# The stages ahead of the expert loop, rearranged: context scaling by halves, order of exponential and weight steps, layer norms moved to ScalarE

## The chip, the core and the metric

The kernel runs on one core of a Trainium2 chip, as one launch. The metric is device time in microseconds (us) of one execution; three executions of the kernel before took 943.69, 947.76 and 951.05 us, median 947.76. TensorE (PE) does matmuls and transposes; VectorE (DVE), ScalarE (ACT) and GpSimd (POOL) do the elementwise work; SyncE (SP) issues transfers (DMA). Each engine works through its own instructions in the order written, and a transfer is queued on the engine that issues it.

## The reference, cut to what matters

`x` is 16 sequences of 256 positions by 256 channels (4,096 rows); `ctx` is 16 sequences of 120 positions by 256 channels. In short, with `LN` a layer norm:

```
h0  = LN(x)
z   = LN(ctx @ W_in + b_in) * g_ln + beta_ln
h   = silu(pe @ Wp1 + bp1) @ Wp2 + bp2            # a filter per channel, 512 taps
w   = exp(-l * exp(a))                            # the window, l = 0..511
cv  = causal_conv(w * h, z) over 512 positions, every second one kept: 256
xr  = h0 + silu(LN1(h0) @ W1a + b1a) @ W1b + b1b  # first MLP, 256 -> 512 -> 256
y   = xr * cv
x   = x + tanh(g_xattn) * (y + silu(LN2(y) @ W2a + b2a) @ W2b + b2b)   # second MLP
h   = LN(x) @ Wm + bm, cut into heads of 32
g   = the two largest of softmax(head @ emb), over 16 experts
out = sum over those two of g * (gelu(head @ W1[e] + b1[e]) @ W2[e] + b2[e])
x   = x + tanh(g_ffn) * (out @ Wo + bo)
```

The reference does the convolution with Fourier transforms, and its result is in fp32.

## The kernel before, in words

**Precision.** The fp32 factors of a product are split into two parts of a faster format: `hi`, a rounded copy, and `lo`, the rest (`f - hi`). A product is three matmuls (hi·hi, hi·lo, lo·hi). Splitting a weight or an activation is therefore one copy and one subtraction; names such as `nt_hi`/`nt_lo`, `s_hi`/`s_lo`, `w_hi`, `v_hi` are these parts.

**Order.** From the start up to `tc.manual_schedule()` (L956) a scheduler with a model of the engines places the instructions; from there on each engine gets them in the order in which the program writes them. Generators are used to interleave: a function yields after each piece, `some(gen, n)` runs the next `n` pieces of it, `whole` runs the rest.

**Front (to 58 us).** Loads go out on the queues of SyncE and ScalarE: `load_ctx` (L623) brings the four pieces of the context, `bc` (L643) holds all row biases, copied to every partition. The exponential of `a`, the two tanh gates and the window follow (L706 to L711), then the filter's small MLP (L712 to L736), which goes to memory as `filt_d`, from where SyncE's `load_hankel` fetches Hankel tiles (`hk`, 1.07 MB each, three buffers). `Context(half).product()` (L752) multiplies eight of the 16 sequences by W_in: four tiles for each half, each with four of the 32 slices (a slice, called a row in what follows, is half the positions of one sequence) and a matmul by `pick_z` for the bias, sums of squares on ScalarE, and a scaling by g_ln on VectorE (Y, `z_sb`). `context_root` (L778) forms the reciprocal root `rz` of all 32 rows, and `context_norm` (L783) scales the 32 rows into `zn`: the first 12 by a ScalarE copy and a GpSimd add, the other 20 each by one operation on VectorE.

**First MLP and convolution (55 to 185 us).** The 4,096 rows are eight jobs (`Mlp1`) of 512. A job has `norms`, `prep` (`prep_n`, the normed rows, and `prep_x`), `turn` (transposes, then the split into `nt_hi`, `nt_lo`), `first` (four tiles: matmuls L205, ScalarE's silu L260, `s_lo` by L268, on VectorE for the last two tiles and on GpSimd for the first two) and `second` (matmuls, from L278; its first one in each job's bias is L293). The convolution is 16 steps: `conv_mm` (64 matmuls L901, two copies `cvs` L908) and `conv_turn` (transposes, and the product with `xr`). `mlps1` (L1057) interleaves, through `mixed` (L1047): at each piece of a job one piece of `weights`, and at every second piece one of `side`, the convolution:

```python
side, weights, since = conv(), chain(early_roots(2, 3), early_roots(3, XB), early_weights(), early_roots(XB, NB)), 0
```

XB is 5 and NB is 8. `early_roots` (L817) takes statistics and roots of the x tiles of later jobs; `early_weights` shifts and splits the second MLP's weights W2a (`w2`) and W2b (`v2`), the tiles x2 to x4 and both weights being loaded on GpSimd's queue behind `m0.first`.

**Up to the experts (142 to 254 us).** `Mlp2` jobs of 512 rows (`prep` L340) and `Route` jobs (`prep` L400, which computes the experts' inputs and gates; `shift`, `lay` and `fetch` carry them through memory into the layout of the experts). Both norm their rows by `normed` (L178): with an `off` on ScalarE, else on VectorE; both have called it without one. `behind_it` (L1167) is the order of the last of this: it spreads `late_weights` (the experts' W1 into `wst`, with two ScalarE copies and two GpSimd subtractions L1038; then the load of Wo into a shared stage, and its split), `routes[1]` and `mlps[2]` over jobs 6 and 7 of the first MLP.

**Expert loop (254 to 945 us).** For each block of rows, TensorE multiplies by W1 (`hps`, L1259), ScalarE applies gelu (`hid`, L1264), TensorE multiplies by W2 (`eo`, L1274), VectorE weights by the gate (`part`, L1282), GpSimd adds (`comb`, L1284). In between stand the second MLP's and the routes' remaining jobs.

Of the kernel before, what the change touches and what calls it, by code (L numbers as in the profile page):

```python
# [24 lines left out]
FP = mybir.dt.float32  # L25
# [8 lines left out]
P = 128  # L34
# [11 lines left out]
NB = 8  # L46
# [47 lines left out]
def block_kernel(  # L94
# [151 lines left out]
    def first(job, bank, w, b, bh, by_table):  # L246

        job.s = []
        for m in range(NM):
            ps = bank("first")  # L250
            project(ps, job, w, m)
            if job.room:
                hi, lo, f = job.room(m)
            else:
                hi, lo = pair(s_in[0], "s", [P, TB], s_in[1])
                f = base.tile([P, TB], FP, name="silu", tag="silu", bufs=2)
            job.s.append((hi, lo))
            if by_table:
                nc.scalar.activation(hi, ps, AF.Silu, bias=b[:, m : m + 1])  # L259
                nc.scalar.activation(f, ps, AF.Silu, bias=b[:, m : m + 1])  # L260
            else:

                nc.scalar.activation(f, ps, AF.Tanh, bias=bh[:, m : m + 1], scale=0.5)
                nc.vector.tensor_scalar(f, f, 0.5, 0.5, ALU.mult, ALU.add)
                nc.vector.scalar_tensor_tensor(f, ps, b[:, m : m + 1], f, ALU.add, ALU.mult)
                nc.vector.tensor_copy(hi, f)
            eng = nc.vector if by_table and m >= NM // 2 else nc.gpsimd
            eng.tensor_tensor(lo, f, hi.bitcast(FP), ALU.subtract)  # L268
            yield 6 * TB
# [47 lines left out]
    class Mlp2:  # L317


        def __init__(self, i, room=None):  # L320
            self.i, self.room = i, room

# [17 lines left out]
        def prep(self, pool=base, name="n"):  # L340
            t0 = 4 * self.i
            self.n = pool.tile([P, 4, D], FP, name=name, tag=name)
            normed(self.n, Y[:, t0 : t0 + 4, :], mv2, t0, self.r)

# [44 lines left out]
    class Route:  # L389
# [9 lines left out]
        def prep(self):  # L399
            t0 = 4 * self.i  # L400
            y = Y[:, t0 : t0 + 4, :]
            self.n = base.tile([P, 4, D], FP, name="n", tag="n")
            normed(self.n, y, mv3, t0, self.r)

# [133 lines left out]
    with ExitStack() as ph:  # L538
# [83 lines left out]

        def load_ctx(g):  # L623
            nc.scalar.dma_start(ctx_sb[g], ctx_r[:, :, bass.ts(g, 4 * P)])

# [14 lines left out]
        for g in (1, 2, 3):  # L640
            load_ctx(g)
        w1a = staged(W1a.rearrange("(c p) n -> p c n", p=P), 2, DFF, nc.sync)
        nc.scalar.dma_start(bc, rows.partition_broadcast(P))  # L643
        w1b = staged(W1b.rearrange("(c p) n -> p c n", p=P), NM, D, nc.sync)
# [59 lines left out]


        ea = scalar("a", AF.Exp)  # L706
        tgx = scalar("g_xattn", AF.Tanh)
        tgf = scalar("g_ffn", AF.Tanh)
        nea = const.tile([P, 1], FP, name="nea")
        nc.vector.tensor_scalar(nea, ea, -1.0, None, ALU.mult)  # L710
        nc.scalar.activation(window, window, AF.Exp, scale=nea)  # L711
        for m, n in enumerate((P, P, DPOS)):  # L712
# [64 lines left out]

        def context_root():  # L778
            var = bank("turn")[:, 0:32]
            nc.tensor.matmul(out=var, lhsT=both, rhs=ss, start=True, stop=True)  # L780
            return rsqrt_eps("rz", var, 32, pool=front)

        def context_norm(rz, by_pool=12):  # L783
            for n in range(32):
                b, k = n // 2, n % 2
                dst = zn[:, :, k, b : b + 2 * B + 1 : 2 * B]
                z, c = z_sb[:, n // 4, n % 4], rz[:, n : n + 1]
                shift = gz[:, 1].rearrange("p (r e) -> p r e", e=2)
                if n < by_pool:
                    nc.scalar.activation(z, z, AF.Copy, scale=c)  # L790
# [3 lines left out]
                else:  # L794
                    nc.vector.scalar_tensor_tensor(
                        dst, z.rearrange("p (r e) -> p r e", e=2), c, shift, ALU.mult, ALU.add
                    )


# [32 lines left out]
        class Mlp1:  # L832
            room = None

# [212 lines left out]
        def mixed(gen, n=9):  # L1047
            nonlocal since
            for _ in range(n):
# [3 lines left out]
                if since % 2 == 0:  # L1053
                    some(side)
                some(weights)

        def mlps1(first, last):  # L1057

            for n in range(first, last):
# [17 lines left out]
                if n < last - 1:  # L1077
                    soon.prep()
                else:
# [3 lines left out]
                    mlp20.stats()  # L1083
                mixed(ahead)
            mlp20.norms()

# [80 lines left out]
        def behind_it():  # L1167
# [447 lines left out]
```

## Time and profile before

| what | value |
| --- | --- |
| median of three executions | 947.76 us (943.69 to 951.05) |
| the profiled execution | 946.54 us, its span 944.7 us |
| TensorE matmul busy | 903.9 us (96%) |
| TensorE weight load busy | 491.3 us (52%) |
| VectorE busy | 713.5 us (76%) |
| ScalarE busy | 670.2 us (71%) |
| GpSimd busy | 566.4 us (60%) |
| transfers | 149.88 MB, mean 159 GB/s |
| mean granted TensorE clock | 0.986 |

All durations in what follows come from that one profiled execution, whose span is the time from the first to the last instruction. A busy engine isn't always one that limits: shares are means over stages, so the span is read stage by stage, and in each the question is which wait ends last. An operation is named by its line in the kernel before, its output tile and its inputs. "Granted clock" is the share of full speed that TensorE was given.

### The profile page before, as it was taken

What the parts mean: (1) busy time and instruction counts of PE and PEld (TensorE: products, weight loads), DVE (VectorE), ACT (ScalarE), POOL (GpSimd) and SP (SyncE); (2) the same over time, 40 slices, a digit from 0 to 9 for tenths busy, and PEclk for the clock granted to TensorE, in tenths of its full rate; (3) what the DMA queues carried; (4) which work ended last, traced back from release to release, by engine and by line L of the source; (5) the groups of instructions that cost most, each with busy time, mean ns of one, the idle gap of its engine ahead of it and who ended that gap; (6) DMA issues with size and microseconds to landing.
All of it is one profiled execution on the core that took longest, in us unless ns stands there. A gap on an engine that the chain in (4) does not pass through costs nothing.

```text
span 944.7 us, 16777 instructions
## 1 busy us (share of the span) xinstructions
PE 903.9 (96%) x6068; PEld 491.3 (52%) x6068; DVE 713.5 (76%) x1297; ACT 670.2 (71%) x856; POOL 566.4 (60%) x459
## 2 busy tenths in 40 slices
PE   6989999998889999999999999999999999989996
PEld 2767778787544544454544445454454444433433
DVE  5676447779978997898899789978985985693343
ACT  4553435585478778778877877887788778778883
POOL 3051222545467677776777777777767867486553
PEclk9999999999799999999999999999999999999998
DMA  7758970352457656947675686469465747746441
GB/s 241 167 155 218 228 203 16 76 137 69 120 134 182 154 149 177 232 128 179 187 198 144 169 213 161 133 188 240 113 182 171 187 127 197 185 117 179 123 123 45
DMA packets 88744, 149.88 MB, mean 159 GB/s; under 512 B 10251, under 2 KB 51723, under 8 KB 88655
## 3 DMA queue, kind: packets, MB, share of 16 engines
q1 hardware_dynamic: 85428, 141.08, 57.3%
q0 software_dynamic: 1296, 4.72, 1.7%
q10 hardware_dynamic: 1936, 3.02, 0.9%
q8 instruction: 48, 0.79, 0.4%
q14 instruction: 36, 0.29, 0.1%
HBM read 120.32 MB, written 28.46 MB: 157 GB/s over the span
## 4 chain that ended last, share of the span: by engine, by line
PE 58%; DVE 20%; DMA 9%; issue 5%; ACT 3%; SPq 2%; POOL 2%; POOLq 0%; ACTq 0%; DVEq 0%
PE hps L1259 20%; PE eo L1274 18%; PE aux L1318 5%; DVE part L1282 4%; DMA gates<-g_d 4%; DMA hk<-filt_d 3%; PE b_second L278 2%; PE b_first L205 2%; PE b_conv L901 2%; PE aux L205 2%; DMA t_d<-t_lo 2%; PE aux L1387 1%; DVE bn L170 1%; PE b_conv L205 1%; ACT hid L1264 1%
## 5 line engine op out<-in xcount | busy, mean ns | idle before, releaser
L1264 ACT ACTIVATE hid<-hps 128x1024 f32<-128x1024 f32 x512 | 512.1, 1025 | 145.0 <-PE hps L1259 132.2
L1284 POOL TENSOR_TENSOR comb<-comb,part 128x512 f32<-128x512 f32 x240 | 329.5, 1373 | 159.4 <-DVE part L1282 154.1
L1259 PE MATMUL hps<-stack,wst 98*128 98x512 f32 x1024 | 341.8, 425 | 2.8 <-ACT hid L1264 2.8
L1259 PEld LDWEIGHTS hps<-stack,wst 98*128 98x128 f32 x1024 | 162.3, 189 | 248.7 <-ACT hid L1264 120.2
L1274 PE MATMUL eo<-hid,w2s 128*32 128x512 f32 x2048 | 274.6, 608 | 7.9 <-DVE part L1282 6.7
L1282 DVE SCALAR_TENSOR_TENSOR part<-eo,cv,gates 128x512 f32<-128x512 f32 x237 | 175.4, 744 | 90.6 <-PE eo L1274 68.8
L1274 PEld LDWEIGHTS eo<-hid,w2s 128*32 128x32 f32 x2048 | 40.6, 108 | 102.9 <-issue 47.5
L268 POOL TENSOR_TENSOR s_lo<-silu,s_hi 128x512 fp32r<-128x512 f32 x18 | 23.0, 1289 | 71.7 <-ACT silu L260 45.0
L1377 POOL TENSOR_TENSOR s_lo<-silu,s_hi 128x512 fp32r<-128x512 f32 x24 | 31.0, 1292 | 33.6 <-DVE s_hi L1376 27.6
L1375 DVE SCALAR_TENSOR_TENSOR silu<-silu,u 128x512 f32<-128x512 f32 x24 | 26.1, 1087 | 22.5 <-ACT u L1372 22.5
L259 ACT ACTIVATE s_hi<-b_first,b1f 128x512 fp32r<-128x512 f32 x32 | 21.9, 684 | 26.0 <-PE b_first L205 25.4
L1409 DVE TENSOR_SCALAR n<-Y,mv,r_r 128x256 f32<-128x256 f32 x44 | 37.2, 886 | 3.0 <-POOL nt_lo L1433 3.0
L278 PE MATMUL b_second<-v_hi,s_hi 128*128 128x256 f32 x144 | 38.6, 300 | 0.0
L278 PE MATMUL b_second<-v_lo,s_hi 128*128 128x256 f32 x144 | 37.1, 289 | 0.0
L901 PE MATMUL b_conv<-hk,zn 60*32 60x256 f32 x1024 | 34.7, 379 | 1.9 <-ACT cvs L908 1.4
L1433 POOL TENSOR_TENSOR nt_lo<-n,nt_hi 128x512 fp32r<-128x512 f32 x26 | 33.6, 1292 | 3.1 <-DVE nt_hi L1432 3.1
L908 ACT COPY cvs<-b_conv 128x256 f32<-128x256 f32 x32 | 10.5, 376 | 30.2 <-PE b_conv L901 30.2
L278 PEld LDWEIGHTS b_second<-v_hi,s_hi 128*128 128x128 f32 x144 | 28.7, 199 | 3.1 <-issue 2.7
L205 PE MATMUL b_first<-nt_hi,w_hi 128*128 128x512 f32 x64 | 27.1, 424 | 2.5 <-ACT silu L260 2.4
L278 PEld LDWEIGHTS b_second<-v_lo,s_hi 128*128 128x128 f32 x144 | 28.8, 200 | 0.4
L1432 DVE CAST nt_hi<-n 128x512 fp32r<-128x512 f32 x26 | 28.5, 1097 | 0.0
L1457 POOL TENSOR_TENSOR Y<-Y,tbo 128x256 f32<-128x256 f32 x28 | 28.1, 1012 | 0.0
(282 smaller groups left out, 1488.4 us busy)
## 6 DMA issues: line engine op xcount, KB each, us to landing
gates<-g_d SPq DMA_DIRECT2D x126, 512.0 KB
hk<-filt_d SPq DMA_DIRECT2D x128, 134.1 KB
stack<-t_d SPq DMA_DIRECT2D x48, 256.0 KB
g_d<-gt SPq DMA_DIRECT2D x32, 256.0 KB
n<-laid_d SPq DMA_DIRECT2D x13, 512.0 KB
laid_d<-laid SPq DMA_DIRECT2D x44, 128.0 KB
xr<-in_x SPq DMA_DIRECT2D x8, 512.0 KB
t_d<-t_hi SPq DMA_DIRECT2D x16, 256.0 KB
```

The costliest lines, as they stand in the source:

```text
L205: nc.tensor.matmul(out=out, lhsT=l, rhs=r, start=(i == 0 and j == 0), stop=(i == n - 1 and j == 2),)
L278: nc.tensor.matmul(out=ps[:, j, :], lhsT=s[k][l][:, c], rhs=v[r][:, k], start=(k == 0 and i == 0 and not (whole and (j or bias))), stop=(k ...
L901: nc.tensor.matmul(out=ps[bass.ts(c, 2 * B), 0:L], lhsT=zn[rows, 4 * n + c, k, e * B : (e + 2) * B], rhs=hk[rows, 2 * c + e, k * SQ : k * ...
L1259: nc.tensor.matmul(out=ps[:, g, :], lhsT=wst[0:KST, e, :], rhs=st[0:KST, 2 * g2 + g, :], start=True, stop=True,)
L1264: nc.scalar.activation(t, ps, AF.Gelu)
L1274: nc.tensor.matmul(out=eo[bass.ts(g, HD)], lhsT=w2s[:, e, :], rhs=hid[g // 2][:, g % 2, :], start=True, stop=True,)
L1282: nc.vector.scalar_tensor_tensor(to, eo, col("b2", e), gs, ALU.add, ALU.mult)
L1284: nc.gpsimd.tensor_tensor(comb, comb, to, ALU.add)
L1318: nc.tensor.matmul(out=ps, lhsT=w[l][:, k, c], rhs=r[:, k], start=(k == 0 and j == 0), stop=(k == 1 and j == 2),)
L1377: nc.gpsimd.tensor_tensor(lo, f, hi.bitcast(FP), ALU.subtract)
L1409: nc.vector.tensor_scalar(job.n[:, j + k, :], Y[:, t0 + k, :], mv[:, t0 + k, 0:1], job.r[:, j + k : j + k + 1], ALU.subtract, ALU.mult,)
L1433: nc.gpsimd.tensor_tensor(lo, src, hi.bitcast(FP), ALU.subtract)
```

## The change

It has eight parts, and what is computed stays the same.

- `load_ctx(1..3)` and the load of `bc` are issued on GpSimd's queue, not ScalarE's.
- The window's exponential stands directly behind exp(a), ahead of the two tanh; its factor `nea` is made on ScalarE, not VectorE.
- `context_root` and `context_norm` work on 16 rows. Half 0 is scaled directly behind its own products, ahead of those of half 1: 5 of its rows by ScalarE and GpSimd, 11 on VectorE. Half 1 is scaled around job 0's first layer: 2 rows by ScalarE and GpSimd, 14 on VectorE, seven before the layer and five behind each of its tiles until they are done.
- In job 0 all four `s_lo` are VectorE's (`by_vector`).
- `early_roots` passes its step on while the x tile isn't loaded, for each tile, and waits six steps more for x5, x6 and x7.
- In `mixed` every other one of the first 24 steps takes two pieces of `weights`, not one.
- In `mlps1` the rows of the job after next are normed (`prep_n`) ahead of the last tiles of the next one's first layer, and `prep_x` comes behind them.
- `Mlp2(i)` and `Route(i)` with i > 0 norm on ScalarE, with an offset from VectorE; in `behind_it`, `wst`'s copies and subtractions go from ahead of `routes[1]`'s norms to behind `lay(a)`, and the load of Wo from ahead of `lay(a)` to ahead of `lay(m)`.

```diff
@@ first @@
-            eng = nc.vector if by_table and m >= NM // 2 else nc.gpsimd
+            eng = nc.vector if by_table and (m >= NM // 2 or job.by_vector) else nc.gpsimd
@@ Mlp2.prep; Route.prep alike, with mv3 @@
-            normed(self.n, Y[:, t0 : t0 + 4, :], mv2, t0, self.r)
+            off = offset(mv2[:, t0 : t0 + 4, 0], self.r, 4) if self.i else None
+            normed(self.n, Y[:, t0 : t0 + 4, :], mv2, t0, self.r, off)
@@ loads @@
-        def load_ctx(g):
-            nc.scalar.dma_start(ctx_sb[g], ctx_r[:, :, bass.ts(g, 4 * P)])
+        def load_ctx(g, queue=nc.scalar):
+            queue.dma_start(ctx_sb[g], ctx_r[:, :, bass.ts(g, 4 * P)])
...
         for g in (1, 2, 3):
-            load_ctx(g)
+            load_ctx(g, nc.gpsimd)
...
-        nc.scalar.dma_start(bc, rows.partition_broadcast(P))
+        nc.gpsimd.dma_start(bc, rows.partition_broadcast(P))
@@ window @@
         ea = scalar("a", AF.Exp)
+        nea = const.tile([P, 1], FP, name="nea")
+        nc.scalar.mul(nea, ea, -1.0)
+        nc.scalar.activation(window, window, AF.Exp, scale=nea)
         tgx = scalar("g_xattn", AF.Tanh)
         tgf = scalar("g_ffn", AF.Tanh)
-        nea = const.tile([P, 1], FP, name="nea")
-        nc.vector.tensor_scalar(nea, ea, -1.0, None, ALU.mult)
-        nc.scalar.activation(window, window, AF.Exp, scale=nea)
@@ context @@
-        def context_norm(rz, by_pool=12):
-            for n in range(32):
+        def context_norm(half, rz, by_pool):
+            shift = gz[:, 1].rearrange("p (r e) -> p r e", e=2)
+            for j in range(16):
+                n = 16 * half + j
                 b, k = n // 2, n % 2
...
-                if n < by_pool:
+                if j in by_pool:
...
+                yield
@@ early_roots @@
-                if i == NB - 1:
-                    while i not in xs:
-                        yield
-                    for _ in range(6):
-                        yield
+                waits = 6 if i >= XB else 0
+                while i not in xs:
+                    yield
+                for _ in range(waits):
+                    yield
@@ front @@
-        for half in range(2):
-            Context(half).product()
-        rz = context_root()
+        Context(0).product()
+        for _ in context_norm(0, context_root(0), range(2, 16, 3)):
+            pass
+        Context(1).product()
+        rz = context_root(1)
...
-        context_norm(rz)
-        for _ in m0.first(bank):
-            pass
+        m0.by_vector = True
+        rest = context_norm(1, rz, range(2))
+        some(rest, 7)
+        for m, _ in enumerate(m0.first(bank)):
+            some(rest, 5)
@@ mixed @@
-                some(weights)
+                some(weights, 1 + (since % 2 if since < 24 else 0))
@@ mlps1 @@
                 if n < last - 1:
-                    soon.prep()
+                    soon.prep_n()
...
                 mixed(ahead)
+                if n < last - 1:
+                    soon.prep_x()
@@ behind_it @@
             a, m = routes[1], mlps[2]
-            some(weights)
             a.norms()
             a.prep()
...
+            lay(a)
             some(weights)
-            lay(a)
             yield
             yield from rest
             m.prep()
             for _ in soon:
                 some(stats_3)
                 yield
+            some(weights)
             lay(m)
```

More of the change, by code (lines that the diff above doesn't have):

```diff
@@ L320, in __init__ @@
         def __init__(self, i, room=None):
-            self.i, self.room = i, room
+            self.i, self.room, self.by_vector = i, room, False
         def stats(self):
@@ L402, in prep @@
             self.n = base.tile([P, 4, D], FP, name="n", tag="n")
-            normed(self.n, y, mv3, t0, self.r)
+            off = offset(mv3[:, t0 : t0 + 4, 0], self.r, 4) if self.i else None
+            normed(self.n, y, mv3, t0, self.r, off)
         def shift(self):
@@ L776, in product, with context_root @@
                     )
[L778 to L781, printed above, removed]
-        def context_norm(rz, by_pool=12):
-            for n in range(32):
+        def context_root(half):
+            c = bass.ts(half, 16)
+            var = bank("turn")[:, 0:16]
+            nc.tensor.matmul(out=var, lhsT=both, rhs=ss[:, c], start=True, stop=True)
+            return rsqrt_eps("rz", var, 16, pool=front)
+        def context_norm(half, rz, by_pool):
+            shift = gz[:, 1].rearrange("p (r e) -> p r e", e=2)
+            for j in range(16):
+                n = 16 * half + j
                 b, k = n // 2, n % 2
                 dst = zn[:, :, k, b : b + 2 * B + 1 : 2 * B]
-                z, c = z_sb[:, n // 4, n % 4], rz[:, n : n + 1]
-                shift = gz[:, 1].rearrange("p (r e) -> p r e", e=2)
-                if n < by_pool:
+                z, c = z_sb[:, n // 4, n % 4], rz[:, j : j + 1]
+                if j in by_pool:
                     nc.scalar.activation(z, z, AF.Copy, scale=c)
@@ L832, in block_kernel @@
         class Mlp1:
-            room = None
+            room, by_vector = None, False
             def __init__(self, i):
```

## The prediction

> **What bounds the kernel now.** First I cut the span into stages, busy time of each engine in each (columns: stretch, length, TensorE, weight loads, VectorE, ScalarE, GpSimd, granted clock, DMA share, GB/s):
>
> ```profile
> 12.70:44.20 31.50, 31.50 (x296) 21.82 (x296) 19.52 (x64) 19.94 (x80) 2.35 (x1) 1.00 0.67 188
> 44.20:58.20 14.00, 11.48 (x52) 8.23 (x51) 13.63 (x36) 9.73 (x22) 9.97 (x17) 0.88 0.25 49
> 82.70:111.00 28.30, 28.30 (x440) 22.02 (x439) 15.01 (x55) 9.82 (x23) 4.58 (x5) 1.00 0.85 224
> 111.00:142.00 31.00, 27.50 (x424) 21.25 (x423) 15.45 (x49) 14.52 (x31) 7.66 (x6) 0.94 0.82 209
> 225.80:245.80 20.00, 17.77 (x110) 15.82 (x109) 19.52 (x37) 8.32 (x13) 11.30 (x7) 0.91 0.51 142
> 254.40:944.70 690.30, 673.24 (x3802) 313.98 (x3800) 535.52 (x791) 538.99 (x569) 480.87 (x365) 0.99 0.62 162
> ```
>
> The expert loop from 254 us on is TensorE's (673 of 690 us); the diff doesn't touch it. Everything happens before. There TensorE is the bound too, except where the waits of TensorE (up to 260 us) name others:
>
> ```profile
> PE b_first L205 <- ACT silu L260: 2.4, 1, 2.4
> PE b_second L293 <- DVE xb L877: 2.1, 1, 2.1
> PE b_turn L235 <- DVE nt_lo L238: 2.0, 1, 2.0
> PE b_conv L901 <- ACT cvs L908: 1.4, 1, 1.4
> ```
>
> The chain of waits shows what stood before the last two, at 106 to 120 us: the split of W2a on VectorE, a norm and a weight cast on ScalarE ahead of the silus, then the late `nt_lo`:
>
> ```profile
> 106.69 0.46 DVE w_hi L126
> ...
> 109.47 1.09 ACT xt L184 x3
> ...
> 111.55 0.57 ACT s_hi L259
> 112.12 0.57 ACT silu L260
> 112.69 0.94 ACT v_hi L988
> ...
> 119.56 0.58 DVE nt_lo L238
> ```
>
> The timeline shows the cost of neighbours on VectorE and GpSimd (a four-column operation is 0.16 us alone and 2.26 us beside the `wst` subtraction), and a convolution step when its Hankel tiles are late (2.89 us) or not (1.96):
>
> ```profile
> 226.23 4.80 POOL L1038 TENSOR_TENSOR wst<-stage,wst 33x1024 fp32r<-33x1024 f32 x2 [1.79 <-issue]
> 226.41 2.26 DVE L157 SCALAR_TENSOR_TENSOR r_t<-r_r 128x4 f32<-128x4 f32 x1
> 231.09 0.16 DVE L159 SCALAR_TENSOR_TENSOR r_r<-r_t,r_r 128x4 f32<-128x4 f32 x1
> 85.37 2.89 PE L901 MATMUL b_conv<-hk,zn 60*32 60x256 f32 x64
> 91.08 1.96 PE L901 MATMUL b_conv<-hk,zn 60*32 60x256 f32 x64
> ```
>
> **Part A, up to the first convolution step (58.2 us): +1.3.** Exponential first removes two table loads of 1.28 us (before L711 and L717) from ScalarE, so the filter and the first Hankel loads come some 4 us sooner; worth nothing itself, since the first three tiles (from 30.9 us) are down long before 58 us, and TensorE has only 0.8 us of gaps from 7.76 to 44 us. The four loads on the GpSimd queue take about 0.8 us each there (L574: 0.75 to 0.79) ahead of its memsets: pick_z, done at 6.5 us, comes near 10; the first product needs it only near 17 in the new order (three L717, two L724 first). They no longer wait for earlier loads (7.26 us for the first now), so they share the engines with Wp1, which TensorE waits for until 7.76: 3 queues for 2 stretch its last 4.7 us by 0 to 1.5; I take 0.7. The row cast of bc now stands before x0's statistics (11.0 us) on VectorE. bc is fourth in its queue; W2b, fifth in such a one, landed after 11.0 us, so bc near 3.5+11.0 = 14.5; behind the cast queue x0's statistics and root and the filter. VectorE has 2.0 and 3.1 us of idle time up to 22 us to absorb that.
>
> Scaling: before, all 32 rows wait for one root (47.7 us); VectorE does 20 in 9.99 us, so 0.50 each. Now it does 11+14 = 25 (+2.5), a second root (10 steps of 0.2, +2.0) and two `s_lo` (0.66 each, +1.3) before the last: +5.8. Against it stands idle time it can fill: the first root needs four tiles (36.5 us), and after that VectorE idles 0.48+1.46+1.64+1.64 = 5.2 between the Y scalings. Net +0.6, with 0.7 from above +1.3. But the 12 ScalarE copies (3.63 us) that hold the silus become two, so L205's 2.4 us wait goes; what is late next is `zn`, so it brings nothing. Ends: -3 to +8, the latter if bc lands with the last early load (x1, 22.4 us) and the VectorE queue shifts by 7.9; I stay near the row of W2b, the same kind of load in the same queue.
>
> "Trainium Kernel Development and Optimization", Key Constraints, in the Trainium skill, speaks against the new queue: transfers from all queues interleave on the same 16 engines, and a further queue saves issue time only. By that rule the 1.5 us stands in place of the 0.7, and the total is 0.8 higher; the DMA share of 0.78 in the first 10 us leaves some 2 us of idle engines, so here it need not.
>
> **Part B, jobs 0 and 1 (55.6 to 111 us): -2.** The long steps at 62.1, 73.4, 85.4 and 97.3 us exceed 1.96 by 0.85, 1.45, 0.93 and 0.27: 3.5. GpSimd's queue has 7 adds (before 12, plus two `s_lo`) ahead of the x2 to x4, W2a and W2b loads, so their 2.5 MB start near 52 instead of 56.4 us, and less of them meets the Hankel loads from 60.3 us. The weight steps moved in (x4's statistics 2.3 us, W2a's split 2.5) lie where VectorE is busy 15.0 of 28.3 us; what waits behind the split is one `nt_lo`, asked for two matmul groups later (1.4+2.5 us). The matmuls of W2a's shift (L214) stay in job 1, but now take a `b_first` bank among its last two silu tiles, up to 1.2 us (one tile's two silus). The new waits on x5 to x7 only pass steps by. Ends +1.2 to -3.5.
>
> **Part C, job 2 (111 to 142): -4.5.** From one L293 to the next: 27.1, 28.3 and 31.1 us. A job is 12.7 us of convolution (five of 1.96+0.59) and 12.6 of its own: 25.3, so job 2 loses 5.8: 3.5 of waits, the rest at half clock (0.94 granted). In the new order the split and the `v2` cast (1.04) run in job 1, and xt's norm (2.08) comes behind the silus, needed only a job later: both are off this path. Late next is VectorE's n (1.38) and the two `s_lo`; I keep 1.3 of the 5.8 for that. Ends -1 to -5.8.
>
> **Part D, mlp21's norm at 184.7: -0.8.** VectorE gives 1.38, gets the offset (0.23); ScalarE, idle 4.7 us until 186.1, takes 2.07, delaying two silus by 0.9. Ends +1 to -1.2.
>
> **Part E, 225.8 to 254: -3.5.** VectorE is full. Without the `wst` subtraction beside it, routes[1]'s root ends near 228 instead of 234.1 (four stretched operations, 7.0 us for 0.7). Its norm (1.38) and mlps[2]'s (2.93) leave for ScalarE, 2.07 each. There routes[1]'s norm waits for the root, and job 7's first silu waits behind it: ready 231.5, needed by 232.4. L293 then goes at 235.2 instead of 237.45. Next late: ScalarE, with the `wst` casts (1.98) and a norm ahead of the third silu, 237.9; TensorE asks for its s_hi near 238.7. `wst` is ready near 239, and Wo near 241: its load now waits on SyncE until GpSimd frees the stage, with laid stores and a fetch behind it, and its ScalarE cast (0.62) stands ahead of the first gelu. Both are just ahead of a loop at 242 instead of 245.8. I take 3.5; ends -6 and +1.
>
> Sum: 1.3-2-4.5-0.8-3.5 = -9.5. The profiled execution took 946.54 (span 944.7), 1.2 under the median of 947.76 of three runs; 937.0 for it, **938.3** for the median.
>
> **Rivals.**
> Supply (0.21): after the first step 13 Hankel tiles of 1.07 MB, x5 to x7 and about 1 MB of the rest follow: 16.4 MB at 224 GB/s are 73 us, against 86.4 us now and 77.1 without the 9.3 of B and C. At 209 GB/s, with all 2.5 MB still behind the first step, it is 86: B and C give nothing, 944.8. For: DMA share 0.82 to 0.95. Against: the longest stalls are not on Hankel tiles.
>
> Clock sooner (0.17): weight loads of L721 fall from 0.34 to 0.19 us only at 21.27, after 13.5 us of broken work. Elsewhere unbroken work was at full rate after 3.0 us (L205 from 45.57) and 3.5 (from 120.18). Now three L717 and two L724 (5.6+2.7 us) are unbroken; full rate after two such stretches, 7 us, saves half of 6.5: -3.3, and with C's end -1.3 more: 933.7. Against: the first run of 3.75 us, two L714, did not lift it.
> "TensorE: Matmul & The Clock Gate", Part 1, in the Trainium skill: one busy window of about 3.4 us, free-running, releases the gate; by that rule this case is the forecast, since 8.3 us hold a whole window wherever it starts. No row here shows whether matmuls on half the rows count as busy, so it stays a rival.
>
> Half clock through the products (0.13, the slow side): the new order starts with matmuls on 64 rows and cuts the full L724 run in two with products between. 26 product matmuls take 3.25 us cold, 32 take 1.97 warm, so a tile costs 4.8 for 2.33. Seven tiles: +17, 955; slower than before from four tiles on (9.5/2.47). Against: once up, the clock held through all products from 23 to 42 us.
>
> Not passed on (0.09): the loop's start is set by something else (a gate load, Wo); D and E vanish, 942.6. For: `wo_hi` waited 1.8 us for its load before. Against: that was well before 245.8.
>
> **Numbers.** The forecast has 0.40, and its own range is 932 to 945. Range 931 to 950, leaving out the half clock and the low tails of forecast and sooner clock. 1% is 9.5 us, about what a measurement of this kernel can tell from no change, and lies at 938.3: faster 0.37 (half of the forecast's 0.40, and the sooner clock's 0.17), slower by that (over 957.2) only when half clock meets limited supply (955+6.5), a late bc, or both: 0.09; same 0.54.
>
> **What would show it.** A right: L205's 2.4 us wait gone, the first convolution step at 59 to 60. B: no such step over 2.3 us. C: L293 to L293 near 27 in job 2, no wait for `nt_lo`. E: routes[1]'s root under 3 us, the first expert matmul near 236.5. Wrong if the products end past 46 us, or the steps stay long.

## The result, and the profile after

The changed kernel takes 934.81 us (median of four executions, 934.53 to 936.37), the kernel before 945.88 (four, 943.69 to 951.05): 11.1 us less, ratio 0.988 with a 95% interval of 0.983 to 0.992. The profiled span fell by 10.1 us, from 944.7 to 934.6.

The stages of the profile after, in the columns of before (stretch, length, TensorE, weight loads, VectorE, ScalarE, GpSimd, granted clock, DMA share, GB/s):

```profile
44.20:58.20 14.00, 13.25 (x99) 9.99 (x106) 12.63 (x42) 7.66 (x15) 4.60 (x7) 0.88 0.44 145
108.70:134.00 25.30, 25.30 (x423) 19.13 (x422) 11.97 (x40) 11.35 (x25) 5.36 (x5) 1.00 0.97 209
212.10:240.40 28.30, 24.09 (x134) 19.73 (x135) 20.84 (x61) 18.28 (x28) 17.41 (x12) 0.90 0.44 121
240.40:934.60 694.20, 676.45 (x3813) 316.04 (x3812) 537.75 (x801) 540.62 (x571) 482.50 (x367) 0.99 0.61 162
```

Job 2 (second line) was 31 us with 27.5 of TensorE and a clock of 0.94; now TensorE is busy in all of its 25.3. Its waits up to 260 us:

```profile
PE b_second L717 <- DMA hk<-in_Wp: 9.7, 1, 9.7
PE hps L1273 <- ACT hid L1278: 2.9, 2, 2.7
...
PE b_first L205 <- DVE nt_lo L238: 1.2, 2, 0.7
...
PE b_first L205 <- ACT silu L260: 0.6, 1, 0.6
```

All four that the prediction quoted are gone: the silu's 0.6 stands at 77.05 us, not at the quoted place in job 0 (52.57 before). Two are longer, the first load Wp1 (before 7.8) and the first gelu of the loop (0.7). Two short waits for `nt_lo` are new, 0.51 us in job 0 and 0.68 at 93.5 us. The chain of waits in job 2, which went over VectorE and ScalarE, is TensorE alone:

```profile
113.32 0.59 PE b_turn L926 x4
...
114.34 1.41 PE b_second L278 x12
115.76 1.89 PE b_conv L908 x64
117.65 0.59 PE b_turn L926 x4
118.23 1.41 PE b_first L205 x6
```

The gain by stage is read from the starts of five TensorE groups: the first convolution step; the bias matmul of the second layer (L293) of jobs 2, 3 and 6; the first W2 product (`eo`) of the expert loop; and the end of the span. "Job 2" is the stretch from its bias matmul to job 3's, and so on for the others.

| stretch | before | after | change | forecast |
| --- | --- | --- | --- | --- |
| S1 start to first convolution step | 58.24 | 57.25 | -1.0 | +1.3 (A) |
| S2 to job 2 | 52.73 | 51.41 | -1.3 | -2 (B) |
| S3 job 2 | 30.99 | 25.40 | -5.6 | -4.5 (C) |
| S4 job 3 to job 6 | 78.05 | 78.00 | 0.0 | -0.8 (D) |
| S5 job 6 to first W2 product | 31.03 | 28.34 | -2.7 | -3.5 (E) |
| the loop | 693.7 | 694.2 | +0.5 | 0 |

### The profile page after: what moved, and what is told of

Its sections match the earlier page's. It is cut to its first block, busy times and chain, and to the rows that moved or that the text cites. A ratio compares the mean times of both kernels' runs of the same rounds, so it can differ in the third digit from the quotient of the medians.

```text
span 934.6 us, 16793 instructions
## 1 busy us (share of the span) xinstructions
PE 897.2 (96%) x6070; PEld 485.9 (52%) x6070; DVE 707.2 (76%) x1304; ACT 673.2 (72%) x862; POOL 565.6 (61%) x456
## 4 chain that ended last, share of the span: by engine, by line
PE 60%; DVE 20%; DMA 8%; issue 6%; POOL 2%; ACT 2%; SPq 2%; POOLq 0%; DVEq 0%; ACTq 0%
PE hps L1273 19%; PE eo L1288 17%; DVE part L1296 5%; PE aux L1332 5%; DMA gates<-g_d 4%; PE b_first L205 4%; PE b_second L278 3%; PE b_conv L908 2%; PE aux L205 2%; DMA hk<-filt_d 2%; DMA t_d<-t_lo 1%; PE b_conv L205 1%; DVE ex L371 1%; DVE d L481 1%; PE b_conv L724 1%
## 5 line engine op out<-in xcount | busy, mean ns | idle before, releaser
L268 POOL TENSOR_TENSOR s_lo<-silu,s_hi 128x512 fp32r<-128x512 f32 x16 | 20.4, 1287 | 68.5 <-ACT silu L260 54.8
L1391 POOL TENSOR_TENSOR s_lo<-silu,s_hi 128x512 fp32r<-128x512 f32 x24 | 31.0, 1293 | 33.6 <-DVE s_hi L1390 27.0
L908 PE MATMUL b_conv<-hk,zn 60*32 60x256 f32 x1024 | 31.8, 378 | 0.0
L915 ACT COPY cvs<-b_conv 128x256 f32<-128x256 f32 x32 | 10.5, 375 | 27.5 <-PE b_conv L908 27.4
```

What stands on the lines that cost most here:

```text
L908: nc.tensor.matmul(out=ps[bass.ts(c, 2 * B), 0:L], lhsT=zn[rows, 4 * n + c, k, e * B : (e + 2) * B], rhs=hk[rows, 2 * c + e, k * SQ : k * ...
L1391: nc.gpsimd.tensor_tensor(lo, f, hi.bitcast(FP), ALU.subtract)
```

## The experiments

e1 to e12 are the changed kernel with something altered (e5 is the kernel before with one part of the change). Each was profiled once and timed beside the kernel before. Executions of one kernel in one session lie 1 to 11 us apart, and the loop, the same in all, took 690.0 to 694.9 us in the profiles: a total can't tell 2 us here, a stage can. The same stretches (us) in all runs but e9, whose profile can't be read beside the others (below):

| run | S1 | S2 | S3 | S4 | S5 | median total | ratio, 95% |
| --- | --- | --- | --- | --- | --- | --- | --- |
| after | 57.25 | 51.41 | 25.40 | 78.00 | 28.34 | 934.81 | 0.983-0.992 |
| e1 | 56.93 | 49.66 | 25.41 | 79.33 | 28.42 | 934.03 | 0.983-0.994 |
| e2 | 57.73 | 56.22 | 25.40 | 77.72 | 29.16 | 941.29 | 0.994-0.999 |
| e3 | 60.86 | 51.21 | 25.40 | 77.74 | 28.29 | 934.90 | 0.985-0.994 |
| e4 | 59.89 | 50.89 | 25.40 | 77.78 | 28.08 | 935.89 | 0.988-0.993 |
| e5 | 57.95 | 51.64 | 26.63 | 78.01 | 31.55 | 942.19 | 0.994-0.998 |
| e6 | 57.41 | 50.98 | 25.40 | 77.89 | 28.11 | 934.82 | 0.987-0.994 |
| e7 | 56.55 | 50.91 | 25.40 | 77.74 | 30.79 | 935.00 | 0.988-0.994 |
| e8 | 58.09 | 50.91 | 25.85 | 78.07 | 29.21 | 935.01 | 0.987-0.993 |
| e10 | 54.76 | 49.36 | 25.40 | 79.14 | 28.91 | 933.37 | 0.983-0.990 |
| e11 | 59.66 | 50.30 | 25.40 | 79.10 | 28.87 | 937.66 | 0.988-0.995 |
| e12 | 54.49 | 50.25 | 25.41 | 79.05 | 27.40 | 934.33 | 0.986-0.990 |

Runs with the changed kernel's code in a stretch show how well it repeats: S1 within 1.6 us (after, e1, e2, e7, e8), S2 to S4 within 0.5, S5 within 1.1 (after, e2, e3, e4, e6). "The first W2 product" is a time from the start of the span.

### e1, e2, e5: what job 2 lost its time to

```diff
 e1
-                some(weights, 1 + (since % 2 if since < 24 else 0))
+                some(weights)
 e2
-                    soon.prep_n()
+                    soon.prep()
...
-                if n < last - 1:
-                    soon.prep_x()
 e5, on the kernel before
-                    soon.prep()
+                    soon.prep_n()
...
                 mixed(ahead)
+                if n < last - 1:
+                    soon.prep_x()
```

> The changed kernel with one piece of the second MLP's weights per step again, instead of up to two; the norm of job 3's rows stays behind the silus. In the changed kernel job 2 (one bias matmul of the second layer to the next) takes 25.40 us, before 30.99. Theory 1 (the split of W2a and the cast of W2b are what stood in job 2): job 2 takes 29 to 31 us, the convolution's copies or nt_lo are waited for again, and the total is 4 to 5.6 us longer, 939 to 940.5. Theory 2 (the norm of job 3's rows ahead of the silus was what stood there): job 2 stays under 26.5 us, total under 936. Theory 3 (each alone is harmless in part, the sum of both overran): between, 27 to 28 us, 936.5 to 938.

> The changed kernel with the whole preparation of the job after next ahead of the last silu tiles again (its x part on ScalarE 2.08 us ahead of the silus); the weights stay sooner. Theory 1 (weights): job 2 stays at 25.4 to 26 us, total 934.8 to 935.5. Theory 2 (norm): job 2 takes 29 to 31 us, and jobs 0 and 1, which have the same order, may also lose up to 2 us each; total 939 to 943. Theory 3 (sum): job 2 27 to 28 us, total 936.5 to 938.

> The kernel before with one part of the change alone: in the first MLP's loop only the rows are normed on VectorE ahead of the last silu tiles, and the x part (2.08 us on ScalarE) comes behind them. The weights stay one piece per step. Theory 1 (e1 and e2: that norm ahead of the silus is what job 2 lost its time to, wherever the weights are): job 2 takes 25.4 to 26.5 us instead of 30.99, the loop's first W2 product comes near 245.5 instead of 251.0, total 938 to 940. Theory 2 (it needs the weights sooner as well): job 2 stays at 29 us or more, total 942 to 944.

e1: job 2 takes 25.41 us, so theory 2: the weights may stand where they were. Moving them brought nothing: without it S2 is 1.75 us shorter, S4 1.3 longer. e2: total as theory 2 has it, but the place is another. Job 2 stays at 25.40; job 0, with the weights in it, takes 32.2 us (bias matmul 55.02 to 87.22) instead of 26.9. Timelines of e2 on VectorE, ScalarE and TensorE (start, duration, engine, line, operation, tile, idle time before and what ended it):

```profile
76.85 0.24 DVE L175 SCALAR_TENSOR_TENSOR off<-mv,r_r 128x8 f32<-128x8 f32 x2
77.01 1.38 DVE L188 TENSOR_SCALAR n<-xt,mv,r_r 128x256 f32<-128x256 f32 x4
77.45 2.07 ACT L184 ACTIVATE xt<-xt,off,r_r 128x256 f32<-128x256 f32 x4 [2.53 <-DVE n L188]
79.43 0.67 ACT L259 ACTIVATE s_hi<-b_first,b1f 128x512 fp32r<-128x512 f32 x1
80.00 0.67 ACT L260 ACTIVATE silu<-b_first,b1f 128x512 f32<-128x512 f32 x1
80.73 0.79 PE L205 MATMUL b_first<-nt_hi,w_hi 128*128 128x512 f32 x1 [3.77 <-ACT silu L260]
```

ScalarE norms x in place, and the profile shows it waiting for VectorE's own norm (n), which reads the same x; the root and the offset of this x were ready at 63.2 us. VectorE came to n at 77.0, behind the root of two later tiles (`off` in the first line). ScalarE stood 2.5 us with the silus queued behind it; TensorE lost 3.77 us, and then ran at half clock (granted 0.50; 0.79 and 0.63 us for a 0.39 us matmul). Job 2 of the kernel before shows the same, there behind the split of W2a (this x's offset was ready at 90.8 us):

```profile
108.36 0.75 DVE L127 SCALAR_TENSOR_TENSOR w_lo<-stage,cv,w_hi 128x512 fp32r<-128x512 f32 x1
109.03 1.38 DVE L188 TENSOR_SCALAR n<-xt,mv,r_r 128x256 f32<-128x256 f32 x4
109.47 2.08 ACT L184 ACTIVATE xt<-xt,off,r_r 128x256 f32<-128x256 f32 x4 [3.55 <-DVE n L188]
```

So job 2 lost its time to two things together, the norm ahead of the silus and VectorE late by the split. Taking either away is enough there (25.41 in e1, 25.40 in e2), but in e2, with weight steps sooner, VectorE is late in job 0 instead; only the norm's place frees both. No run norms x into a tile of its own, so that the read alone is what held ScalarE is read from the traces, not tested. e5 confirms it from the other side: this one part on the kernel before brings S3 from 30.99 to 26.63, and 5.3 us by the first W2 product (251.04 to 245.78). Its total, 942.19 against 945.20 beside it, lies in theory 2's range, 2 us above theory 1's; the stages agree with theory 1, and the ratio's interval (0.994 to 0.998) still holds the 5.3 us that they say.

### e3, e6: the front's loads and the exponential

```diff
 e3
-            load_ctx(g, nc.gpsimd)
+            load_ctx(g)
...
-        nc.gpsimd.dma_start(bc, rows.partition_broadcast(P))
+        nc.scalar.dma_start(bc, rows.partition_broadcast(P))
 e6
-        nea = const.tile([P, 1], FP, name="nea")
-        nc.scalar.mul(nea, ea, -1.0)
-        nc.scalar.activation(window, window, AF.Exp, scale=nea)
         tgx = scalar("g_xattn", AF.Tanh)
         tgf = scalar("g_ffn", AF.Tanh)
+        nea = const.tile([P, 1], FP, name="nea")
+        nc.vector.tensor_scalar(nea, ea, -1.0, None, ALU.mult)
+        nc.scalar.activation(window, window, AF.Exp, scale=nea)
```

> The changed kernel with the context pieces 1 to 3 and the row biases on ScalarE's queue again. The first matmul, at 9.72 us in the changed kernel and 7.73 before, waits for Wp1. Theory 1 (three queues shared the engines, and Wp1 paid 1.96 us for it; TensorE is the bound from there to the convolution): first matmul at 7.7 to 8.2, the products end at 41.5 to 42.3 instead of 44.9 minus the two us of thin matmuls (43.0), total 933.3 to 934.3. Theory 2 (what the row biases and the late context pieces release on VectorE and GpSimd comes later in turn): first matmul sooner, but gaps in the products of over 1 us, total 935 to 938.

> The changed kernel with the two tanh and VectorE's factor ahead of the window's exponential again; the loads stay on GpSimd's queue. In e3, with the loads on ScalarE's queue, ScalarE's first operation came at 9.9 us instead of 3.85, the exponential at 16 behind the silus with two more table loads, and TensorE stood 2.8 us for the third silu; the first convolution step came at 60.86 instead of 57.25. Theory 1 (the queue did all of that, ScalarE has time from 3.85 us on): first step at 57 to 57.7, total 934.5 to 935.5. Theory 2 (the order is needed too, since the factor from VectorE comes behind its mean subtractions at 8.7 us): the silus' table is loaded twice again, first step at 58.5 to 61, total 936 to 938.5.

e3 starts sooner, as both theories had it (7.84 us), and then loses it and more, as theory 2: TensorE stands 2.8 us among the products, and the first convolution step comes at 60.86, 3.6 us later. ScalarE and TensorE in e3:

```profile
9.88 1.28 ACT L657 ACT_TABLE_LOAD   x1 [9.88 <-DMA gz<-in_rows_z]
14.77 1.28 ACT L712 ACT_TABLE_LOAD   x1
16.07 0.72 ACT L712 ACTIVATE hk<-hk,nea 128x512 f32<-128x512 f32 x1
20.59 2.08 ACT L184 ACTIVATE xb<-xb,off,r_r 128x256 f32<-128x256 f32 x4 [3.80 <-DVE n L188]
23.62 1.28 ACT L720 ACT_TABLE_LOAD   x1
25.65 2.76 PE L724 MATMUL b_conv<-hk 64*128 64x512 f32 x4 [2.80 <-ACT hk L720]
```

and ScalarE after:

```profile
3.85 1.28 ACT L657 ACT_TABLE_LOAD   x1 [3.85 <-DMA cv<-in_cols]
5.84 0.72 ACT L712 ACTIVATE hk<-hk,nea 128x512 f32<-128x512 f32 x1
```

With the loads in its queue ScalarE begins to compute at 9.9 us, when the first products already want silus, and the exponential falls between two of these, with a table load on each side. Between it and the third silu (at 24.9 us) also stands x0's norm, which waited 3.80 us for VectorE; what each of these adds to TensorE's 2.8 us wasn't tested apart. Freed at 3.85 it has the exponential done by 6.6. e6 shows that the order written is worth nothing that S1 can show once the queue is free (57.41 against 57.25): theory 1. The gain that the change's words give to the exponential is the queue's. The total of e3 (934.90, just under theory 2's range) does not show its 3.1 us at the first W2 product (243.50 against 240.40); its profiled loop, at 691.7, was 2.5 us shorter, which is within the loop's spread.

### e4: scaling in one piece

```diff
-        Context(0).product()
-        for _ in context_norm(0, context_root(0), range(2, 16, 3)):
-            pass
-        Context(1).product()
-        rz = context_root(1)
+        for half in range(2):
+            Context(half).product()
+        rz = context_root()
...
-        m0.by_vector = True
-        rest = context_norm(1, rz, range(2))
-        some(rest, 7)
-        for m, _ in enumerate(m0.first(bank)):
-            some(rest, 5)
+        for _ in context_norm(rz, range(12)):
+            pass
+        for _ in m0.first(bank):
+            pass
```

> The changed kernel with one root and one scaling of all 32 context rows again (12 by ScalarE and GpSimd, 20 by VectorE, two of job 0's subtractions on GpSimd). Theory 1 (the scaling by halves gained in this stage and nowhere else): the wait of L205 for a silu of 2.4 us is back, the first convolution step at 58.5 to 59.5 instead of 57.25, total 936 to 937. Theory 2 (GpSimd's queue is what mattered: with 12 adds ahead the loads of x2 to x4, W2a and W2b start some 4 us later, and meet the Hankel tiles): as theory 1, and convolution steps over 2.3 us are back between 60 and 100 us, another 1 to 2.5 us: 937.5 to 939.5. Theory 3 (it brought nothing): 934.5 to 935.3.

Theory 1, a little more: the wait for the silu is back (1.9 us), the first step comes at 59.89, and no step is over 2.3 us, though the loads of x2 to x4, W2a and W2b start at 56.5 us as before (56.4; after 50.1). So their earlier start is not what shortened the steps; by the first W2 product 1.6 us are left of the 2.6. VectorE's scaling in e4 and after:

```profile
47.88 9.95 DVE L800 SCALAR_TENSOR_TENSOR zn<-Y,rz_r,gz 128x128 f32<-128x128 f32 x20
```

```profile
40.50 4.09 DVE L801 SCALAR_TENSOR_TENSOR zn<-Y,rz_r,gz 128x128 f32<-128x128 f32 x11
48.73 1.92 DVE L801 SCALAR_TENSOR_TENSOR zn<-Y,rz_r,gz 128x128 f32<-128x128 f32 x5
51.80 1.50 DVE L801 SCALAR_TENSOR_TENSOR zn<-Y,rz_r,gz 128x128 f32<-128x128 f32 x5
53.73 1.23 DVE L801 SCALAR_TENSOR_TENSOR zn<-Y,rz_r,gz 128x128 f32<-128x128 f32 x4
```

On average a row takes VectorE 0.50 us in e4 and 0.30 to 0.38 after. Cut into 0.05 us stretches, e4's trace shows the rows 0.45 us apart while GpSimd adds (48.4 to 53.9 us), 1.3 us apart beside its two `s_lo` subtractions (to 56.5), and 0.25 to 0.3 behind them. e4 brings back both, the adds and the subtractions.

### e7, e8: the last stretch ahead of the loop

```diff
 e7
             a, m = routes[1], mlps[2]
+            some(weights)
             a.norms()
...
-            lay(a)
             some(weights)
+            lay(a)
...
-            some(weights)
             lay(m)
 e8, in Mlp2 and in Route
-            off = offset(mv2[:, t0 : t0 + 4, 0], self.r, 4) if self.i else None
+            off = None
```

> The changed kernel with the copies and subtractions of wst ahead of routes[1]'s norms again, and the load of Wo ahead of its laying down. In the changed kernel routes[1]'s root takes 2.0 us, job 7's bias matmul comes 15.1 us after job 6's, and the first gelu of the loop waits until 236.33 for the split of Wo, 2.7 us of TensorE. Theory 1 (two effects of like size, the stretched root against the late Wo): the root takes 6 to 8 us, job 7's bias matmul comes 1.5 to 2.5 us later, TensorE's wait for the first gelu shrinks to under 1 us; the loop's first W2 product 0 to +1 us from 240.4, total 934.5 to 936. Theory 2 (the root's place is all that counts): first W2 product at 242.5 or later, total 937 to 938.5. Theory 3 (Wo is all that counts): 238 to 239.5, total 932.5 to 934.

> The changed kernel with the second MLP's and the routes' norms on VectorE for all, as before. Stage of mlp21 (160 to 190 us): it gained nothing (7.90 us ahead at 142 us and 7.95 at 220), so nothing is lost there in either theory. Theory 1 (with wst behind, VectorE has 3.5 us of idle time and the norms fit on either engine): job 7's bias matmul within 0.7 us of 227.17, first W2 product 240.4 to 241, total 934.5 to 935.5. Theory 2 (VectorE is the bound there): routes[1]'s norm and mlps[2]'s come back ahead of job 7's xb and s_lo, 1.4 to 3 us, total 936 to 938. Theory 3 (ScalarE is what binds now): 0.5 to 2 us sooner, total 932.8 to 934.3.

e7: the root is stretched to 6.4 us, and job 7's bias matmul comes 20.08 us behind job 6's instead of 15.11 (before 17.44): 5.0 us, twice what was expected. The wait for the gelu falls from 2.7 to 0.7, so S5 is 2.45 us longer, between theories 1 and 2 (the first W2 product comes at 241.39, since S1 to S4 were 1.5 us shorter). ScalarE's norms make the late root worse than before, since job 7's silus queue behind a norm that waits for it. VectorE and GpSimd in e7:

```profile
217.03 2.26 DVE L157 SCALAR_TENSOR_TENSOR r_t<-r_r 128x4 f32<-128x4 f32 x1
219.33 2.34 DVE L158 TENSOR_TENSOR r_t<-r_t,r_ve 128x4 f32<-128x4 f32 x1
221.70 0.17 DVE L159 SCALAR_TENSOR_TENSOR r_r<-r_t,r_r 128x4 f32<-128x4 f32 x1
216.85 4.79 POOL L1049 TENSOR_TENSOR wst<-stage,wst 33x1024 fp32r<-33x1024 f32 x2 [1.79 <-issue]
```

The two subtractions end near 219.25 and 221.64, and VectorE's two operations at 219.29 and 221.67: each ends with a whole instruction of GpSimd. "SBUF — State Buffer", Terms, in the Trainium skill says this of the port pair that the two engines share, an exclusive lock held for the full instruction; this trace agrees, with 2.3 us for 0.17. e8: job 7's bias matmul keeps its place (15.15 us behind job 6's), yet the first W2 product comes 0.9 us later: `mlps[2]`'s norm on VectorE takes 6.68 us beside wst's subtractions. Since e2, with the code of after there, has the same S5, the 0.9 us isn't shown, and theories 1 and 2 stay open. In S4 nothing changes (78.07), as expected.

### e9, e10, e12: what is late next

```diff
 e9 (with e1's edit)
+        t_wo = early.tile([P, 4, D], FP, name="xb", tag="xb", bufs=XB - 2)[:, 0:2]
+        nc.sync.dma_start(t_wo, Wo.rearrange("(c p) n -> p c n", p=P))
         jobs[6].norms()
...
             a, m = routes[1], mlps[2]
+            halves(wo, t_wo)
 e10, in addition
+        warm = front.tile([P, P], FP, name="warm", bufs=1)
+        nc.vector.memset(warm, 0.0)
+        for n in (7, 1):
+            ps = bank("second").rearrange("p (j d) -> p j d", j=4)
+            for k in range(n):
+                nc.tensor.matmul(out=ps, lhsT=warm, rhs=warm.unsqueeze(1).to_broadcast([P, 4, P]),
+                                 start=(k == 0), stop=(k == n - 1))
 e12, in addition
             for _ in jobs[7].second(bank):
-                some(stats_3)
                 yield
```

> The changed kernel with one piece of weights per step (as e1) and Wo loaded into a free x buffer behind job 5 and split ahead of routes[1]'s norms, so that neither its load nor its split stands between the last wst piece and the first gelu. In the changed kernel TensorE waits 2.7 us for that gelu (before 0.7), and from job 6's bias matmul to the loop's first W2 product it is 28.34 us. Theory 1 (the late Wo is what took back part of the gain): the wait falls to 0.7 us, that stretch to 26 to 26.8, total 931 to 933. Theory 2 (what is late next, job 7's rows or the gates' load, holds the first gelu or W2 product to the same time): the stretch stays at 27.5 to 28.5, total 933.5 to 934.5.

> e9 with eight matmuls of zeros on all 128 rows ahead of everything, while TensorE waits for Wp1 (until 9.7 us); their results are never used. In the changed kernel the clock rose only at some 19.5 us, 9.8 us after the first matmul, though TensorE was busy without a break: 5.6 us of matmuls on 64 rows, then 4 us on 128. Theory 1 (a stretch of full work of some 3.4 us raises the clock, matmuls on 64 rows keep it): L717 takes 2.8 to 3.5 us for its 5.64, the products end 3 to 5 us sooner than e9's, total 927 to 930. Theory 2 (matmuls on 64 rows do not count as work for the clock): it falls again during L717 or in the gap ahead of it, and rises near 19 to 20 us as without: products end within 1 us of e9's, same total. Theory 3 (the zeros run into the first product): L717 starts at 10.5 us or later, total 0 to 1 us longer than e9's.

> e10 with the last statistics of the second MLP's rows taken out from between job 7's second layer on VectorE, to stand behind it. In e10 the first gelu's wait fell to 0.8 us, but the loop's first W2 product stood 1.76 us until 237.57, and VectorE's sum of job 7 (xb), which frees the bank, ended at 237.48, behind 3.1 us of such statistics. Theory 1 (that sum is what is late next): it ends 2.5 to 3.1 us sooner relative to the loop's first product, the stand is gone or under 0.5 us, from the loop's first W1 product to its first W2 product it takes 4.4 to 5 us instead of 6.22; total 1 to 2 us under e10's, 931 to 932.5. Theory 2 (the gates' load or the laid rows hold it): that stretch stays at 5.7 us or more, and the total is e10's, 932.8 to 933.8. In both, ahead of the kernel changed as a whole: by 2 to 4 us with theory 1, 1 to 2 with theory 2.

e9 took 934.09, 934.98, 938.49 and 1,075.19 us. Its profile is that of the last, at a mean granted clock of 0.752, so its stages can't be read beside the others; the other three all lie above theory 1's total, and Wo is read from e10. There the gelu's wait is 0.8 us, but the first W2 product stands 1.76 us for another reason: S5 is 28.91, theory 2's side. e12 finds it: with the statistics behind job 7's sum, that sum ends at 234.8 instead of 237.5, the stand is gone, and from the first W1 product to the first W2 product it is 4.75 us instead of 6.22. The sum was late next, theory 1, though e12's total (934.33) lies above that theory's range.

e10's zeros: the weight loads of the zeros (L609) and of the first products (L726) on TensorE,

```profile
1.06 0.50 PEld L609 LDWEIGHTS b_second<-warm 128*128 128x128 f32 x2 [1.06 <-DVE warm L605]
...
3.79 0.34 PEld L609 LDWEIGHTS b_second<-warm 128*128 128x128 f32 x1 [0.52 <-issue]
4.52 0.19 PEld L609 LDWEIGHTS b_second<-warm 128*128 128x128 f32 x1 [0.40 <-issue]
10.30 0.19 PEld L726 LDWEIGHTS b_second<-hk 64*128 64x128 f32 x1 [0.24 <-issue]
```

and after, without them:

```profile
10.71 0.33 PEld L717 LDWEIGHTS b_second<-hk 64*128 64x128 f32 x1 [0.52 <-issue]
18.02 0.34 PEld L757 LDWEIGHTS b_turn<-bz,pick_z 128*128 128x128 f32 x1 [0.52 <-issue]
20.79 0.30 PEld L724 LDWEIGHTS b_conv<-hk 128*128 128x128 f32 x2 [0.17 <-issue]
```

Full rate (0.19, 0.15 each in the last line) comes 3.5 us after the first zero matmul, and the 64-row products behind it still run at it: the products end 3.7 us sooner (39.34 against 43.01), theory 1 for the clock. 2.5 us of it reach the first convolution step; the total, 933.37, shows little of it, far from the 927 to 930 expected. The sum of all three, e12, is 3.8 us ahead of the changed kernel at the first W2 product (236.60 against 240.40), but its median is 934.33 us, ratio 0.986 to 0.990: no version was shown to beat the change. Why less than those 3.8 us shows in six timed executions (931.97 to 937.25) stays open; the profiled loop, 693.6 us, was not longer.

### e11: one-column matmuls among the products

```diff
-        for _ in shift_through(bank("first"), w1a, "be1", "b1a", b1f):
-            pass
...
         for _ in context_norm(0, context_root(0), range(2, 16, 3)):
             pass
+        for _ in shift_through(bank("first"), w1a, "be1", "b1a", b1f):
+            pass
         Context(1).product()
```

> e9 with the eight pairs of one-column matmuls of W1a's shift (L214, 1.95 us, at 43.0 us in the changed kernel) amid the second half's products instead of behind them. In the changed kernel the clock is at a half from 46.97 to 50.4 us, in the window that follows them, and the eight matmuls of job 0's first layer there take 0.63 us for 0.39. Theory 1 (one-column matmuls with the root's gap behind them are what lowers the clock): the half clock is gone, or lies among the products, and the first convolution step comes 1 to 2.5 us sooner relative to the end of the products; total 929.5 to 932. Theory 2 (the gap at the root is enough, or the thin matmuls lower it where they are): the first step comes within 0.7 us of e9's, total the same.

A miss: the first convolution step comes at 59.66 instead of 57.25, total 937.66 us (ratio 0.988 to 0.995). The half clock moved with the matmuls (stretches of e11; granted clock is third from last):

```profile
32.00:34.00 2.00, 2.00 (x21) 1.88 (x17) 1.90 (x9) 1.28 (x9) 0.00 (x0) 1.00 0.88 218
36.00:38.00 2.00, 2.00 (x17) 1.67 (x17) 1.57 (x9) 0.00 (x0) 0.00 (x0) 0.50 1.02 228
40.00:42.00 2.00, 2.00 (x22) 1.83 (x18) 2.00 (x6) 1.56 (x5) 1.53 (x4) 0.50 1.00 231
```

The one-column matmuls, 32.12 to 34.07, are followed by half clock from about 35.3 to 42 us though TensorE is never idle there, and the gap at the root (1.3 us, up to 48.20), which now has none of them ahead of it, is followed by none. Both theories allowed for that place; neither had the time that half clock costs there.

## Why the prediction was right, and where its terms were not

The time, its direction and the main term (C) held: the forecast was -9.5 in the profile, -10.1 was measured, and 934.81 us lies in the likeliest case's own range. That the sum is so close is partly luck. Up to the first W2 product A and C came out 3.4 us better than forecast and B, D and E 2.3 worse, and the loop alone varies by 5 us. Whether the gain is over 1%, to which the prediction gave 0.37, isn't settled: it is 1.2%, with an interval of 0.8 to 1.7.

- **A** was not the loss that was forecast: +1.3, against -1.0 measured. Five profiles with this front have the first step at 56.55 to 58.09, two with the front before at 58.24 and 57.95 (e5), and the forecast at 59 to 60; so the loss is refuted, and a gain is barely shown. The end of the products was right (+0.7 forecast, +0.8), though Wp1 came 1.96 us later beside the third queue, of which 1.2 came back behind it, with fewer gaps and the full clock sooner. Mis-sized was the scaling: 0.50 us a row was read beside GpSimd's adds and subtractions, which the change removes or moves; after, all 25 rows take 8.74 us, where 20 took 9.99. So the last row is done at 54.96, well ahead of the first step, and the silu's wait, given away in the sum, counts: the first step is 2.6 us later in e4. The prediction gave the two table loads to the exponential's order; e3 and e6 show that they hang on the queue. "Trainium Kernel Development and Optimization", Key Constraints, in the Trainium skill has a further queue save issue time only, on shared engines; the trace agrees with both halves, Wp1 1.96 us later and ScalarE free 6 us sooner, and the second was worth more.
- **B**: right in size (-1.3 for -2), not in mechanism. The convolution steps' excess did fall, from 3.5 to 0.5 us (one step of 2.42 is left, at 84.6), but not by the earlier loads that the prediction named: in e4 these start as late as before and no step is long, with its first step 1.65 us later than before. Which part removed the long steps stays open. The weight steps, priced at nothing, gave up to 1.75 us back (e1).
- **C**: the size was somewhat low (all 5.6 us went, not 4.5), and the two reasons were not a sum: each alone frees job 2 (e1, e2), and moving the weights alone only shifts the loss to job 0 (e2). The norm's place is the part that gains (e5). What made the norm dear was, beside its own 2.08 us, its wait of 3.55 us for VectorE's reading of the same x behind the split, which the prediction did not name.
- **D** brought nothing: neither profile has a wait of TensorE for that norm (at 184.7 us before, 177.3 after); idle time of another engine was counted as gain.
- **E**: job 7's bias matmul came 2.33 us sooner (forecast 2.25), by the root as said. The first W1 product came sooner than forecast (233.63 for 236.5): 2 us of that are the stages ahead, and from job 6's bias matmul it is 21.57 us instead of 25.76, so 4.2 less where 3.5 were taken. But Wo, which was put "just ahead" of the loop, was just behind: it landed at 234.33, TensorE's wait for the first gelu grew by 2.0 us, and 1.5 of the 4.2 were gone again at the first W2 product. That is the rival "Not passed on" in part.

Of the other rivals, supply did not bind (steps of 1.96 us at a DMA share of 0.97), half clock through the products did not happen, and the clock rose between 18.4 and 20.8 us instead of 20.8 to 21.3, while that rival needed it 7 us after the first matmul, near 16.7.

## What to carry to other kernels

An in-place operation on one engine has to wait until another engine has read the same tile, and all that is queued behind it waits too (here 3.55 us before and 2.5 in e2): put it behind the work that the bounding engine asks for next. Take the price of an operation from a row with the neighbours that it will have, not those that the change removes. When a wait is removed just ahead of a phase, list what else ends within 2 us of it (here a load, its split and a bank to be freed), since these are what is late next.

## What the runs showed of the hardware

Matmuls on 64 rows did not raise TensorE's clock: after, 5.6 us of them without a break (from 9.72) stayed at 0.33 us a weight load, 0.34 was still read at 18.02, 8.3 us after the first, and full rate came between 18.4 and 20.8 us, 3 to 5.5 us after the first 128-row matmul. With 128 rows from the start it rose 3.5 us (e10) and 6.1 us (e12, at 7.14) after the first. It then held through 3.5 and 3.0 us of 64-row matmuls; whether it would through more of them isn't shown. "TensorE: Matmul & The Clock Gate", Part 1, in the Trainium skill has a free-running window of about 3.4 us that must be busy; e10 and e12 agree with it, and the forecast's doubt whether half-row work counts as busy was justified. Sixteen one-column matmuls in 1.95 us were followed by half clock (granted 0.50) that began 0.9 to 2.0 us behind their end: from 45.1 us before, 47.0 after, and 35.3 in e11, where they were moved. The granted clock in the profile's columns reads 1.00 through all of the slow start (8 to 20 us before and after), so there the weight loads have to be read instead.
